# Two layers of a graph network on one core: g and y in one room, 64 bytes apart, and the start addresses of y and W modulo 512 bytes

## The chip, the cores and the metric

The kernel runs on one core of one Trainium2 chip. The time is the device time of one execution in microseconds; a kernel's figure is the median of several executions. Beside it there is one profiled execution, whose span runs from the first to the last instruction of the program. TensorE is called PE, VectorE DVE, ScalarE ACT, GpSimd POOL and SyncE SP, as in the profile.

## The reference

The input x has 64 batches of 256 rows and 512 features; adj is one 256 x 256 matrix of zeros and ones for all batches. There are two layers, each with a layer norm, a ReLU and a residual:

```
h   = relu(layernorm(x))
q, k, v = h @ Wq.T, h @ Wk.T, h @ Wv.T
rel = adj.T * (q @ k.T)                  # 256 x 256 for each batch
rel = rel / norm(rel, axis=2)            # each row by its length
x   = x + rel @ v

h   = relu(layernorm(x))
x   = x + (adj @ h) @ weight + bias
```

All of it is float32.

## The kernel before

**Arithmetic.** Every product of float32 operands is made of three passes: an operand is split into an upper part u, a lower part l and a third s, and a product is u by u, plus l by l, plus s by s, with a scaling of the bank by ScalarE (line 354, or 670 for the first pair) between the second pass and the third. A room of parts is therefore three tiles, such as `w_u`, `w_l`, `w_s`. The transform q times k is folded: m is the product of Wq and Wk, made once, and g = m times h, so that the scores are g times h.

**Stages.** Two batches (512 rows) make one pair, and there are 32 pairs; all loops are unrolled in Python. For one pair, in the kernel's own names:

- G (`g_stage`): g from m and h, 48 matmuls of 512 columns. The result is split into the parts of `gy`.
- V (`v_stage`): v from h and wv, 48 matmuls of 512 columns. The result goes into the rooms `v_low` and `late`.
- scores: g and h, 48 matmuls of 256 columns. VectorE multiplies the bank with the turned adj (line 433), and ScalarE takes the sums of squares (line 438).
- attend: the turned scores (`rel`) and the parts of v, 24 matmuls of 512 columns.
- gather: y = adj times the second layer's h, 32 matmuls of 256 columns. The result is split (lines 267 to 270) into the parts of `gy`, where g was.
- mix: y and W, 48 matmuls of 512 columns, onto a bank that ScalarE has filled with the bias (line 347).

Gather and mix belong to the pair before: in step i the order on PE is G(i), V(i), scores(i), gather(i-1), the rest of V(i), mix(i-1), attend(i). The last step has mix(i-1) behind attend(i), and then gather(i) and mix(i).

**Order.** `unit` puts two passes of a product on PE and hands the third to the next unit, so that the third pass stands behind the first two of the product that follows. A stage's first matmuls therefore alternate with the last ones of the stage ahead. Each piece of work goes to a `Plan` with its engine, a cost, and keys that it reads and writes; `Plan.order` works out due times back from PE's sequence and sorts every engine's work by a list schedule. The order is then fixed, and the framework sets the semaphores from the regions of the tiles that each instruction reads or writes.

**Operands.** Each matmul has a left operand, which is loaded into the array by an instruction of its own (a row PEld in the profile), and a right operand, which streams through it. `mm(out, left, right, first)` on line 248 issues both. In G the left operand is m and the right one h, in V h and wv, in scores g and h, in attend rel and v, in gather the second layer's h and adj, in mix y and W.

**Places.** The rooms are laid one behind the other in each partition, each size rounded up to 32 bytes. Most rooms are whole multiples of 512 bytes. In this text the place of an operand is its start modulo 512 bytes, counted from the start of `m`, `wv`, `h`, `v_low`, `late` and `rel`, which all have place 0. The small rooms (`ones`, `low_max`, `low_any`, the statistics and `norms`) take 928 bytes, and a filler makes this 1088, so that the rooms laid behind it stand at place 64; a second filler brings later rooms back to place 0:

```
    room("behind", 40)
    w_p = parts_room("w", DC, D)
    wq_sb, wk_sb = room("wq_sb", DC, D, tag="gy_u"), room("wk_sb", DC, D, tag="gy_l")
    gy_s = room("gy_s", DC, T, dtype=F32R)
    room("level", 112)
```

So before the change W, g and y all have place 64, the turned adj has place 448 (line 698 starts it 64 bytes ahead of a multiple), and every other operand has place 0. Within each of the kernel's tiles one 128-column block is 512 bytes, so an operand's place does not change with the block that is read.

Of the kernel before, what the change touches and what calls it, by code (L numbers as in the profile page):

```python
# [10 lines left out]
F32R = mybir.dt.float32r  # L11
I32 = mybir.dt.int32
# [101 lines left out]
def kernel(  # L114
# [12 lines left out]
    P = 128  # L127
    B, N, D = x.shape
    DC = D // P
    NC = N // P  # L130
    NB = 2
    TC = NB * NC
    T = NB * N
# [6 lines left out]
    pool = ctx.enter_context(tc.tile_pool(name="pool", bufs=1))  # L140
    ps_m = ctx.enter_context(tc.tile_pool(name="ps_m", bufs=1, space=bass.MemoryType.PSUM))

    def room(name, *shape, dtype=F32, tag=None):
        return pool.tile([P, *shape], dtype, name=name, tag=tag or name)

    def parts_room(name, *shape, tag=None):
        return [room(f"{name}_{k}", *shape, dtype=F32R, tag=f"{tag or name}_{k}") for k in "uls"]
# [8 lines left out]
    def hp(k, d):  # L156
        return h[k][:, d] if k < 2 else h_s[d // 2][:, d % 2]
    adj_low = room("adj_low", 2, D, tag="rel_u")
    v_low = room("v_low", 4, D, dtype=F32R)
    blocks = room("blocks", TC, DC, P)  # L160
    h_rel = room("h_rel", TC, D)
    bias_bc = room("bias_bc", D)
    wv_sb, w_sb = blocks.rearrange("p c d n -> p c (d n)"), ring[1]
    ident = room("ident", P)
    ones = room("ones", 1)
    wq_last, wk_last = room("wq_last", D), room("wk_last", D)
    low_max, low_any = room("low_max", 1), pool.tile([1, 1], I32, name="low_any")

    rooms = {}

# [32 lines left out]
    def place(plan, src, dst, keys_in, name, lands, early=0.0):  # L203
        width = src.shape[1] // J
        for j in range(J):
            for k in range(J):
                plan.add("SP", 0.65, lambda j=j, k=k: SP.dma_start(
                    out=dst[ts(j, S), ts(k, width)], in_=src[ts(k, S), ts(j, width)]),
                    keys_in, [(name, j, k)], lands=lands, early=early)

    stats = [
        [
            (room(f"st{j}{n}", TC, 6), room(f"mv{j}{n}", TC, 2), room(f"rs{j}{n}", TC), room(f"nb{j}{n}", TC))
            for n in range(2)
        ]
        for j in range(2)
    ]
    norms = [room(f"rn{n}", NB, NC) for n in range(2)]

    room("behind", 40)
    w_p = parts_room("w", DC, D)
    wq_sb, wk_sb = room("wq_sb", DC, D, tag="gy_u"), room("wk_sb", DC, D, tag="gy_l")
    gy_s = room("gy_s", DC, T, dtype=F32R)
    room("level", 112)

    V, A, G, SP = nc.vector, nc.scalar, nc.gpsimd, nc.sync
    count = {"bank": 0}
# [20 lines left out]
    MM, HALF = 0.231, 0.1185  # L250
# [3 lines left out]
    def split_right_ps(plan, ps, key, parts, names, at, cost=0.49):  # L254
        key = key if isinstance(key, list) else [key]
        u, l, s = ((lambda p=p: p(at)) for p in parts)
        ku, kl, ks = names
        plan.add("ACT", cost, lambda: A.activation(u(), ps, AF.Copy, scale=NEAR), key, ku)  # L258
        plan.add("DVE", 0.63, lambda: V.scalar_tensor_tensor(  # L259
            s(), f(u()), ONE, ps, op0=ALU.mult, op1=ALU.subtract), [*key, *ku], ks)  # L260
        plan.add("DVE", 0.6, lambda: V.scalar_tensor_tensor(  # L261
            l(), f(s()), -CROSS, f(u()), op0=ALU.mult, op1=ALU.add), [*ku, *ks], kl)
# [123 lines left out]
    def gy_half(b):  # L386
        return lambda k, d: [("gy_" + "uls"[k], d, b)]

    def gy_both(d):
        return [[("gy_" + k, d, b) for b in range(NB)] for k in "uls"]  # L390

# [2 lines left out]
    def g_stage(plan, i):  # L394
        for e in range(DC):
            first, second = three(
                lambda k, d, e=e: m_p[k][:, d, ts(e, P)], hp,
                named("m_u", "m_l", "m_s"), h_named, MM)
            unit(plan, first, second, lambda ps, key, e=e: split_right_ps(
                plan, ps, key, [lambda at, q=q: q[:, at, :] for q in gy],  # L400
                gy_both(e), e))

    held = []
# [14 lines left out]
    def scores(plan, i):  # L418
        rn = norms[i % 2]
        for b in range(NB):  # L420
            def outs_of(ps, k, d, b=b):
                return [
                    (ps[:, ts(n, N)], gy[k][:, d, ts(b * NC + n, P)], hp(k, d)[:, ts(b, N)])
                    for n in range(NC)
                ]
            first, second = three(None, None, gy_half(b), h_named, 2 * HALF, outs_of)

            def drain(ps, key, b=b):
                dst = plain[:, b].rearrange("p k (t j s) -> p k t j s", t=NC, j=J) if by_pe(i) else rel[:, b]

                def columns(part):
                    return part.rearrange("p (k t j s) -> p k t j s", k=NC, t=NC, j=J)
                plan.add("DVE", 0.6, lambda: V.tensor_mul(
                    *(part.rearrange("p k t j s -> p (k t) j s") for part in (
                        dst, columns(ps), columns(f(adjt[0]).rearrange("p k m -> p (k m)")))),),
                    [key, "adjt"], [("h_rel", b)])
                for k in range(NC):
                    plan.add("ACT", 0.53, lambda k=k: A.activation(
                        columns(ps)[:, k], dst[:, k], AF.Square, accum_out=rn[:, b, k : k + 1]),
                        [("h_rel", b)], [key, (f"rn{i % 2}", b, k)])  # L440
            unit(plan, first, second, drain)
# [91 lines left out]
    def gather(plan, i, exact):  # L533
        right = adjt[0]
        for b in range(NB):
            for d0 in range(0, DC, 2):
                def first(ps, b=b, d0=d0):
                    def go():
                        for m in range(NC):
                            c = b * NC + m  # L540
                            lefts = [late(3 + 2 * c + k) for k in range(2)] if exact else [
                                changing("late", "h2", 8, D)[:, c]]
                            for n, left in enumerate(lefts):
                                for d in range(2):
                                    mm(ps[:, ts(d, N)], left[:, ts(d0 + d, P)], right[:, m, :],
                                       d == 0 and m == 0 and n == 0)
                    needs = ["adjt", *(
                        ("late", r) for m in range(NC) for c in [b * NC + m]
                        for r in ((3 + 2 * c, 4 + 2 * c) if exact else (4 + c,)))]
                    yield 8 * HALF if exact else 8 * 0.216, go, needs  # L550

                def drain(ps, key, b=b, d0=d0):
                    split_left_ps(
                        plan, ps.rearrange("p (d n) -> p d n", d=2), key,
                        [lambda at, q=q: q[:, d0 : d0 + 2, ts(b, N)] for q in gy],
                        [[(f"gy_{k}", d0, b), (f"gy_{k}", d0 + 1, b)] for k in "uls"], None)
                unit(plan, first, None, drain)

    def mix(plan, i, blocks_of=range(4)):
        slot = i % 2  # L560
        for c in blocks_of:
            b = c // NC
            first, second = three(
                lambda k, d, c=c: gy[k][:, d, ts(c, P)], lambda k, d: w_p[k][:, d, :],
                gy_half(b), named("w_u", "w_l", "w_s"), MM, fresh_bank=False)

            def drain(ps, key, c=c):
                plan.add("DVE", 0.6, lambda: V.tensor_add(
                    ring[slot][:, c, :], ps, ring[slot][:, c, :]), [key], [(f"x{slot}", c)])
                if i + 1 == NP:  # L570
                    plan.add("SP", 0.65, lambda: SP.dma_start(
                        out=outs[i][:, c, :], in_=ring[slot][:, c, :]), [(f"x{slot}", c)], [], lands=3.0)
            unit(plan, first, second, drain, on=bias_bc)
# [53 lines left out]

    with tc.manual_schedule(engines=in_order):
        before_pairs()
    gy = [*(room(f"gy_{k}", DC, T, dtype=F32R) for k in "ul"), gy_s]  # L630
    rel_p = [room(f"rel_{k}", NB, NC, NC, P, dtype=F32R) for k in "ul"]
    adjt = []
    inexact = nc.values_load(low_any[0:1, 0:1], min_val=0, max_val=P * 0xFFF)
# [27 lines left out]
    def first_g(plan):  # L661

        banks = [next_bank() for _ in range(DC)]
        for k in range(3):
            for e, (ps, key) in enumerate(banks):
                def go(e=e, k=k, ps=ps):
                    for d in range(DC):
                        mm(ps, m_p[k][:, d, ts(e, P)], hp(k, d), k == 0 and d == 0)
                if k == 2:
                    plan.add("ACT", 0.49, lambda ps=ps: A.activation(ps, ps, AF.Copy, scale=ONE), [], [key])  # L670
                plan.add("PE", 4 * MM, go, [
                    *((("m_u", "m_l", "m_s")[k], d) for d in range(DC)), *((("h_u", "h_l", "h_s")[k], d) for d in range(DC))], [key])
        for e, (ps, key) in enumerate(banks):
            split_right_ps(plan, ps, key, [lambda at, q=q: q[:, at, :] for q in gy], gy_both(e), e)

    def turn_wv(plan):
        for d in range(DC):
# [105 lines left out]
```

## Time and profile before

| | |
|---|---|
| median of 3 runs | 1564.24 us (1563.73 to 1565.1) |
| the profiled execution | 1564.82 us, span 1563.0 us |
| PE busy | 1550.2 us, 99% of the span, 8046 matmuls |
| DVE busy | 1355.9 us, 87% |
| ACT busy | 1022.5 us, 65% |
| POOL busy | 24.4 us, 2% |
| DMA engines | 98 GB/s on average |
| granted PE clock | 1.0 |

A line of the timeline has the start in us from the span's start, the duration in us, the engine, the line of the kernel, the operation, and its tiles as output<-operands, with "xN" where N neighbours are merged into one line. In the names of this profile the right operand stands first: `bank<-w_u,gy_u` is a matmul of mix, with y as its left operand. All matmuls but the few transposes stand on line 248, the helper `mm`, so a stage is known by its tiles: `m_` with `h_` or `hs` is G, `wv_` is V, `gy_` with `h_` is scores, `rel_` is attend, `adjt` is gather and `w_` with `gy_` is mix. The duration of a merged line is not a sum that can be added to the next start, because matmuls overlap in the record; the difference of two starts is used instead.

### The profile page before, as it was taken

To read this page: it belongs to the slowest core of one execution; us is meant where nothing else is said; L and a number is where in the kernel's file an instruction comes from. 1 tells how busy PE (TensorE), PEld (TensorE's weight loads), DVE (VectorE), ACT (ScalarE), POOL (GpSimd) and SP (SyncE) were. 2 spreads that over 40 slices of the span, in tenths; PEclk is the share of its full clock that TensorE was granted. 3 is DMA by queue.
4 is the path that set the end of the run, shared out by engine and by line. 5 is a ranking of instruction groups with operands and counts; after the bars stand their busy time and mean duration, and the time that the engine had idled before them with its cause. 6 is when DMAs were issued, how large, how long until landed. Compare 5 with 4: busy or idle time off the path is not lost.

```text
span 1563.0 us, 22543 instructions
## 1 busy us (share of the span) xinstructions
PE 1550.2 (99%) x8046; PEld 1322.6 (85%) x8046; DVE 1355.9 (87%) x2419; ACT 1022.5 (65%) x1941; POOL 24.4 (2%) x39
## 2 busy tenths in 40 slices
PE   8999999999999999999999999999999999999998
PEld 5788888888888888888888888888888888888886
DVE  6997889898889988898988899888989888988776
ACT  5567666676667676666676676766666766666654
POOL 0000000000000000000000000000000000000000
PEclk9999999999999999999999999999999999999999
DMA  5321333223333223333223332233332233322211
GB/s 197 113 82 42 121 111 120 71 75 112 117 114 119 64 77 119 113 117 87 73 98 118 111 122 68 77 114 114 115 108 70 80 122 111 119 69 77 86 55 56
DMA packets 91112, 153.63 MB, mean 98 GB/s; under 512 B 17136, under 2 KB 32240, under 8 KB 90992
## 3 DMA queue, kind: packets, MB, share of 16 engines
q1 hardware_dynamic: 80768, 116.46, 24.7%
q0 software_dynamic: 8432, 32.51, 5.8%
q10 hardware_dynamic: 1792, 3.15, 0.6%
q8 instruction: 65, 1.06, 0.3%
q14 instruction: 55, 0.45, 0.1%
HBM read 70.78 MB, written 33.55 MB: 67 GB/s over the span
## 4 chain that ended last, share of the span: by engine, by line
PE 95%; DVE 3%; DMA 0%; ACT 0%; issue 0%; DVEq 0%
PE bank L248 95%; DMA fresh<-in_x_dram 0%; DVE late_parts L259 0%; DVE late_parts L261 0%; DVE rel_s_parts L459 0%; DVE st L285 0%; DVE gy_l L268 0%; DVE rel_l L464 0%; DVE wv_l L261 0%; DVE m_l L261 0%; DVE ht L315 0%; DVE wv_s L259 0%; DVE m_s L259 0%; DVE w_l L261 0%; DVE h_l L332 0%
## 5 line engine op out<-in xcount | busy, mean ns | idle before, releaser
L354 ACT ACTIVATE bank<-bank 128x512 f32<-128x512 f32 x572 | 333.1, 582 | 312.2 <-PE bank L248 307.7
L248 PE MATMUL bank<-wv_s,hs 128*128 128x512 f32 x512 | 138.6, 392 | 0.0
L248 PE MATMUL bank<-w_u,gy_u 128*128 128x512 f32 x512 | 138.0, 391 | 0.0
L248 PE MATMUL bank<-wv_u,h_u 128*128 128x512 f32 x512 | 137.6, 390 | 0.0
L248 PE MATMUL bank<-w_l,gy_l 128*128 128x512 f32 x512 | 137.4, 390 | 0.0
L248 PE MATMUL bank<-w_s,gy_s 128*128 128x512 f32 x512 | 137.2, 390 | 0.0
L248 PE MATMUL bank<-wv_l,h_l 128*128 128x512 f32 x512 | 136.9, 389 | 0.0
L248 PE MATMUL bank<-h_l,m_l 128*128 128x512 f32 x512 | 136.6, 389 | 0.1
L248 PE MATMUL bank<-h_u,m_u 128*128 128x512 f32 x512 | 136.5, 389 | 0.0
L248 PE MATMUL bank<-hs,m_s 128*128 128x512 f32 x512 | 136.3, 389 | 0.0
L259 DVE SCALAR_TENSOR_TENSOR gy_s<-gy_u,bank 128x512 fp32r<-128x512 f32 x128 | 86.3, 676 | 43.0 <-ACT gy_u L258 43.0
L248 PEld LDWEIGHTS bank<-w_u,gy_u 128*128 128x128 f32 x512 | 96.0, 188 | 20.8
L248 PEld LDWEIGHTS bank<-w_l,gy_l 128*128 128x128 f32 x512 | 96.1, 188 | 20.7
L248 PEld LDWEIGHTS bank<-h_l,m_l 128*128 128x128 f32 x512 | 96.0, 188 | 20.4 <-DVE h_l L332 0.5
L248 PEld LDWEIGHTS bank<-wv_l,h_l 128*128 128x128 f32 x512 | 96.1, 188 | 20.2
L248 PEld LDWEIGHTS bank<-h_u,m_u 128*128 128x128 f32 x512 | 96.0, 188 | 20.2 <-ACT m_u L258 0.2
L248 PEld LDWEIGHTS bank<-w_s,gy_s 128*128 128x128 f32 x512 | 96.0, 188 | 20.3 <-ACT bank L354 0.2
L248 PEld LDWEIGHTS bank<-hs,m_s 128*128 128x128 f32 x512 | 96.1, 188 | 19.9
L248 PE MATMUL bank<-adjt_r,late_parts 128*128 128x256 f32 x896 | 112.6, 277 | 0.0
L248 PEld LDWEIGHTS bank<-wv_s,hs 128*128 128x128 f32 x512 | 93.8, 188 | 19.3 <-ACT bank L354 0.9
L248 PEld LDWEIGHTS bank<-wv_u,h_u 128*128 128x128 f32 x512 | 93.7, 188 | 17.8
L248 PEld LDWEIGHTS bank<-adjt_r,late_parts 128*128 128x128 f32 x896 | 107.3, 188 | 0.0
(110 smaller groups left out, 3071.7 us busy)
## 6 DMA issues: line engine op xcount, KB each, us to landing
fresh<-in_x_dram SPq DMA_DIRECT2D x31, 1024.0 KB, 5.7
blocks<-h_rel SPq DMA_DIRECT2D x496, 64.0 KB, 2.0
x_ring<-in_x_dram SPq DMA_DIRECT2D x31, 1024.0 KB, 7.8
out_dram<-x_ring POOLq DMA_DIRECT2D x31, 1024.0 KB, 5.4
h_rel<-h_rel SPq DMA_DIRECT2D x464, 32.0 KB, 1.8
x_ring<-in_L_gnn_weight_dram SPq DMA_DIRECT2D x1, 1024.0 KB, 12.8
blocks<-in_L_gnn_Wv_dram ACTq DMA_DIRECT2D x1, 1024.0 KB, 10.8
out_dram<-x_ring SPq DMA_DIRECT2D x4, 256.0 KB, 2.3
```

What stands on the lines that cost most here:

```text
L248: nc.tensor.matmul(out, left, right, start=first, stop=True, skip_group_check=True)
L259: plan.add("DVE", 0.63, lambda: V.scalar_tensor_tensor(s(), f(u()), ONE, ps, op0=ALU.mult, op1=ALU.subtract), [*key, *ku], ks)
L354: plan.add("ACT", 0.49, lambda: A.activation(ps, ps, AF.Copy, scale=ONE), [], [key])
```

## The change

- The parts of W are laid directly behind `h_rel`, at place 0.
- Each of the three `gy` rooms gets 16 more elements (64 bytes). y is the view from the room's start, at place 0; g is the view from element 16 on, at place 64. `as_y` and `as_g` make these views of a flat tile, and `gy` is no longer used as an operand by name, but as `y_p` and `g_p`.
- The statistics, `norms`, `ones` and `low_max` are laid between the `gy` rooms, so that each `gy` room starts at place 0 again; `bias_bc`, `ident` and the last rows of Wq and Wk follow `gy_s` and move by 96 bytes in place. The filler `behind` is gone and `level` is smaller; the rooms laid behind it keep their addresses.
- Because g and y now overlap with a shift, a block of y covers a part of two blocks of g. Gather's split gets extra keys `g_u`, `g_l` and `g_s`, and scores reads them beside `gy_`, so that the plan knows that a block of y waits for both halves of g that it covers.

No instruction is added or removed, and no shape changes.

```diff
+    wv_sb, w_sb = blocks.rearrange("p c d n -> p c (d n)"), ring[1]
+    BEHIND = 16
+    w_p = parts_room("w", DC, D)
+
+    def as_y(tile):
+        return tile[:, : DC * T].rearrange("p (d t) -> p d t", d=DC)
+
+    def as_g(tile):
+        return tile[:, BEHIND : BEHIND + DC * T].rearrange("p (d t) -> p d t", d=DC)
...
+    wq_room = room("wq_sb", DC * T + BEHIND, tag="gy_u")
+    stats = [norm_rooms(0)]
+    norms = [room(f"rn{n}", NB, NC) for n in range(2)]
+    wk_room = room("wk_sb", DC * T + BEHIND, tag="gy_l")
+    stats.append(norm_rooms(1))
+    ones, low_max = room("ones", 1), room("low_max", 1)
+    gy_s = room("gy_s", DC * T + BEHIND, dtype=F32R)
+    wq_sb, wk_sb = as_y(wq_room), as_y(wk_room)
...
+    room("level", 104)
...
-    room("behind", 40)
-    w_p = parts_room("w", DC, D)
-    wq_sb, wk_sb = room("wq_sb", DC, D, tag="gy_u"), room("wk_sb", DC, D, tag="gy_l")
-    gy_s = room("gy_s", DC, T, dtype=F32R)
-    room("level", 112)
...
+    def g_half(b):
+
+        return lambda k, d: [(name + "uls"[k], d, b) for name in ("gy_", "g_")]
...
-                plan, ps, key, [lambda at, q=q: q[:, at, :] for q in gy],
+                plan, ps, key, [lambda at, q=q: q[:, at, :] for q in g_p],
...
-                    (ps[:, ts(n, N)], gy[k][:, d, ts(b * NC + n, P)], hp(k, d)[:, ts(b, N)])
+                    (ps[:, ts(n, N)], g_p[k][:, d, ts(b * NC + n, P)], hp(k, d)[:, ts(b, N)])
...
-            first, second = three(None, None, gy_half(b), h_named, 2 * HALF, outs_of)
+            first, second = three(None, None, g_half(b), h_named, 2 * HALF, outs_of)
...
-                        [lambda at, q=q: q[:, d0 : d0 + 2, ts(b, N)] for q in gy],
-                        [[(f"gy_{k}", d0, b), (f"gy_{k}", d0 + 1, b)] for k in "uls"], None)
+                        [lambda at, q=q: q[:, d0 : d0 + 2, ts(b, N)] for q in y_p],
+                        [[(f"gy_{k}", d, b) for d in (d0, d0 + 1)] + [
+                            (f"g_{k}", *((d, 0) if b else (d - 1, 1))) for d in (d0, d0 + 1)] for k in "uls"], None)
...
-                lambda k, d, c=c: gy[k][:, d, ts(c, P)], lambda k, d: w_p[k][:, d, :],
+                lambda k, d, c=c: y_p[k][:, d, ts(c, P)], lambda k, d: w_p[k][:, d, :],
...
-    gy = [*(room(f"gy_{k}", DC, T, dtype=F32R) for k in "ul"), gy_s]
+    gy = [*(room(f"gy_{k}", DC * T + BEHIND, dtype=F32R) for k in "ul"), gy_s]
+    g_p, y_p = [as_g(part) for part in gy], [as_y(part) for part in gy]
```

More of the change, by code (lines that the diff above doesn't have):

```diff
@@ L161, with norm_rooms @@
     h_rel = room("h_rel", TC, D)
+    wv_sb, w_sb = blocks.rearrange("p c d n -> p c (d n)"), ring[1]
[5 more added lines that the diff above has]
+        return tile[:, BEHIND : BEHIND + DC * T].rearrange("p (d t) -> p d t", d=DC)
+    def norm_rooms(j):
+        return [(room(f"st{j}{n}", TC, 6), room(f"mv{j}{n}", TC, 2), room(f"rs{j}{n}", TC), room(f"nb{j}{n}", TC))
+                for n in range(2)]
+    wq_room = room("wq_sb", DC * T + BEHIND, tag="gy_u")
[6 more added lines that the diff above has]
+    wq_sb, wk_sb = as_y(wq_room), as_y(wk_room)
+    low_any = pool.tile([1, 1], I32, name="low_any")
     bias_bc = room("bias_bc", D)
-    wv_sb, w_sb = blocks.rearrange("p c d n -> p c (d n)"), ring[1]
     ident = room("ident", P)
-    ones = room("ones", 1)
     wq_last, wk_last = room("wq_last", D), room("wk_last", D)
-    low_max, low_any = room("low_max", 1), pool.tile([1, 1], I32, name="low_any")
+    room("level", 104)
     rooms = {}
@@ L209, in place @@
                     keys_in, [(name, j, k)], lands=lands, early=early)
[L211 to L218, printed above, removed]
-    room("behind", 40)
-    w_p = parts_room("w", DC, D)
-    wq_sb, wk_sb = room("wq_sb", DC, D, tag="gy_u"), room("wk_sb", DC, D, tag="gy_l")
-    gy_s = room("gy_s", DC, T, dtype=F32R)
-    room("level", 112)
     V, A, G, SP = nc.vector, nc.scalar, nc.gpsimd, nc.sync
@@ L673, in first_g @@
         for e, (ps, key) in enumerate(banks):
-            split_right_ps(plan, ps, key, [lambda at, q=q: q[:, at, :] for q in gy], gy_both(e), e)
+            split_right_ps(plan, ps, key, [lambda at, q=q: q[:, at, :] for q in g_p], gy_both(e), e)
     def turn_wv(plan):
```

## The prediction

> **What bounds the kernel now.** I read the page first: the busy shares, the granted clock and the chain that ended last.
>
> ```profile
> PE 1550.2 (99%) x8046; PEld 1322.6 (85%) x8046; DVE 1355.9 (87%) x2419; ACT 1022.5 (65%) x1941; POOL 24.4 (2%) x39
> ...
> PEclk9999999999999999999999999999999999999999
> ...
> PE 95%; DVE 3%; DMA 0%; ACT 0%; issue 0%; DVEq 0%
> ```
>
> PE is busy 99% of the span at full clock and makes 95% of the chain. VectorE is next, at 87%, with idle time in every step. So the time is the sum of the distances between the starts of successive matmuls, and the question is whether the change alters any of those distances. Next I read the timeline of PE over one whole step, of 47.5 us.
>
> ```profile
> 782.62 1.07 PE L248 MATMUL bank<-hs,m_s 128*128 128x512 f32 x4
> ...
> 793.50 1.07 PE L248 MATMUL bank<-wv_s,hs 128*128 128x512 f32 x4
> ...
> 808.30 1.07 PE L248 MATMUL bank<-wv_s,hs 128*128 128x512 f32 x4
> 809.20 1.09 PE L248 MATMUL bank<-w_u,gy_u 128*128 128x512 f32 x4
> 810.13 1.09 PE L248 MATMUL bank<-w_l,gy_l 128*128 128x512 f32 x4
> 811.05 1.10 PE L248 MATMUL bank<-wv_s,hs 128*128 128x512 f32 x4
> 811.98 1.09 PE L248 MATMUL bank<-w_u,gy_u 128*128 128x512 f32 x4
> 812.91 1.07 PE L248 MATMUL bank<-w_l,gy_l 128*128 128x512 f32 x4
> ...
> 819.26 1.07 PE L248 MATMUL bank<-w_s,gy_s 128*128 128x512 f32 x4
> 820.16 0.62 PE L248 MATMUL bank<-v_low,rel_u 128*128 128x512 f32 x2
> ...
> 821.08 1.08 PE L248 MATMUL bank<-w_s,gy_s 128*128 128x512 f32 x4
> 822.00 0.61 PE L248 MATMUL bank<-v_low,rel_u 128*128 128x512 f32 x2
> ...
> 826.08 1.07 PE L248 MATMUL bank<-h_u,m_u 128*128 128x512 f32 x4
> ```
>
> The reader is to take differences of starts. From 782.62 to 793.50 there are 12 groups of four, or 48 matmuls in 10.88 us: 226.7 ns each. G passes into V in this stretch, so both operands change rooms, and no distance grows. All of these operands have place 0. From 812.91 to 819.26, inside mix, 7 groups of four take 6.35 us: again 226.8 ns each. There both operands have place 64. What costs more is the passage between the two places. V's third pass at 808.30 still takes 0.90 us, the first two groups of mix 0.93 and 0.92, the late V group among them 0.93, and the group after that again 0.93, against 0.907 for four at 226.7 ns. Where mix meets attend, 821.08 to 822.00 takes 0.92. From attend to the next G, which share place 0, nothing is added.
>
> **What the Trainium skill says.** Perfetto Trace Analysis, section Tensor Engine Instruction (MATMUL, LD_WEIGHTS), says that a matmul's end in the profile is estimated. The 1.07 us of a group beside a distance of 0.907 agrees, so I use starts alone. TensorE: Matmul & The Clock Gate, in Wait — 56ns, not 53.3ns?, gives 215.7 ns from start to start for 512 columns at full clock. The trace has 226.7, which decides. The same page, under Step-by-step: what each phase is for, says that loading the next weights takes no read bandwidth from the running matmul, through a second port. The trace does not fit this fully: the distance depends on where the operands stand. No page that I found states a rule on places modulo 512 bytes, so the cost comes from the trace alone.
>
> **The change part by part.**
>
> *Mix at place 0.* The step from 809.20 to 826.08 holds 12 groups of four from mix, one of V and 22 matmuls of attend, 74 in all. At 226.7 ns they would take 16.77 us; they take 16.88. The excess is 0.107 us, from the unrounded starts. About 0.08 of it lies in the passage from V, and about 0.025 in the passage to attend. I took the same sum for every step: 30 steps have mix between V and attend. 27 of them give 0.107 to 0.108 us, and three give less, 0.101, 0.093 and 0.083: in these PE was held shortly before mix. Together they come to 3.2 us. With y and W at place 0, these passages become of the kind that G to V is, at no excess. All of this is on PE, on the path. **Minus 3.2 us.**
>
> *The last step* has mix behind attend. Its entry into mix at 1530.95 and the attend group within cost 0.05 us over 226.7 ns each. Then gather and mix alternate; over their own undisturbed distances (113.3 and 226.7 ns) these cost 0.2 us, and a passage from place 0 to gather at 448 and back remains (from gather to V it costs 0.015 us). I take half: 0.1, with 0 and 0.2 as ends. **Minus 0.15 us in all.**
>
> *What stays.* In scores g at 64 meets h at 0, as before, at 117.6 ns for 256 columns; gather's operands keep 0 and 448. The passages from V to scores, and from gather to V, are untouched. No more is to be had there: zero.
>
> *The parts of the small rooms.* `ident`, `bias_bc` and the last rows of Wq and Wk move by 96 bytes in place. `ident` streams through PE 60 times in the whole kernel (groups of 16, 24, 16 and 4). If each cost what the dearest passage matmul does, 240 against 226.7 ns, that is 13 ns by 60, or 0.8 us; at the beginning PE waits for others, and such a loss lies partly beside those waits. The lower end is a gain of about as little. I take zero, with plus 0.8 and minus 0.2 as ends. ScalarE's reads of `bias_bc`, and the splits' writes, take 588 and 590 ns now at places 0 and 64, so no cost of a place shows there: zero.
>
> *The waits from the overlap.* y of rows b and block d covers g of the other half too. So the split of gather's first unit must now wait until scores of b=1 has read its g. The first two passes of it stand before gather on PE, so u and l wait for nothing new. The third pass stands from 800.98 to 801.92, and the writer that needs it is the third part, L269.
>
> ```profile
> 802.19 0.69 DVE L433 TENSOR_TENSOR h_rel<-bank,adjt_r 128x512 f32<-128x512 f32 x1 [1.10 <-PE bank L248]
> 803.41 0.69 DVE L268 TENSOR_TENSOR gy_l<-bank,gy_u 128x512 fp32r<-128x512 f32 x1 [0.53 <-ACT gy_u L267]
> ...
> 805.22 1.27 DVE L269 SCALAR_TENSOR_TENSOR gy_s<-gy_l,bank 128x512 fp32r<-128x512 f32 x2
> ...
> 807.01 1.29 DVE L268 TENSOR_TENSOR gy_l<-bank,gy_u 128x512 fp32r<-128x512 f32 x2
> ```
>
> VectorE's row 433 has waited for that same pass and stands 3 us ahead of 805.22 on the same engine, so the new wait is met before it is reached: zero. In the plan the third part could start two operations (0.49 and 0.6 us) behind gather's end, and the third pass of scores costs 0.95 us there, so no order should move. G's split over the y of the pair before is likewise behind PE work that its own bank already waits for. If the cover were gone, what is queued behind is the splits of v and then mix's first groups at 809.20.
>
> **The sum.** Minus 3.2, minus 0.15, plus 0, is minus 3.3 us. The profiled execution would go from 1564.82 to 1561.5. It stands 0.6 above the median of the runs, 1564.24, and all terms are differences on PE, so I take them from the median: **1560.9 us**. For this kernel 0.2%, which is 3.1 us, is about what a measurement can tell from no change; the forecast lies just beyond that.
>
> **The rivals.** *The passage stays in part or whole.* The excess may belong to the change of rooms or to a third pass that alternates with another product, not to the place. For it: each excess sits at such a seam. Against it: G's seams with V and with attend have the same alternation, change the same number of rooms and cost 0 to 1 ns in all. If only the entry from V goes, the gain is 30 by 0.08, 2.4 us: 1561.8. If only the seam with attend goes, it is 30 by 0.025: 1563.5. If nothing goes, because the rooms don't come to lie where the text says, 1564.2. The rooms' sizes, rounded up to 32 bytes, come out even at W and each gy room, so I hold that unlikely.
>
> *Slower: the flat room is tracked as one piece.* If a write of one block of y waited for a read of another block of the same part, ScalarE's fourth split (L267) would wait for VectorE's third L268. It starts ahead of it now:
>
> ```profile
> 806.86 0.60 ACT L267 ACTIVATE gy_u<-bank 128x512 fp32r<-128x512 f32 x1
> 807.34 0.60 ACT L354 ACTIVATE bank<-bank 128x512 f32<-128x512 f32 x1
> ```
>
> The third L268 begins at 807.01 and runs 0.65 to 0.69, so the split would begin at about 807.7, 0.8 us late, and the scaling behind it (L354) would end at 808.8, where V's third pass on PE wants it at 808.30. PE would lose 0.5 us in each of 30 steps: plus 15, less 3.3, gives 1576. It decides from a delay of about 0.35 us on, the time between the scaling's end at 807.94 and 808.30. Against it: each block is a region of its own, and even if a strided block counted from its first to its last byte, the fourth split's stretch would not touch the third's, as they cover different blocks d.
>
> **How the numbers follow.** That the passages go whole: 0.80; the gain is then 3.1 to 3.6 us, and two thirds of it, with the runs' own spread of 1.4 us, lies beyond 3.1. In part: 0.08. Not at all: 0.05. Slower: 0.07. So faster by over 0.2%: 0.8 by 0.67 and a little, 0.55; within 0.2%: 0.27 from the main case and 0.11 from the two rivals with the smaller gain, 0.38; slower 0.07. The range goes from 1559.8 (3.6 and the runs' spread) to 1562.6, which takes in the partial case and the bound on `ident`; about 0.17 is left out.
>
> **What would show it.** In the timeline of PE the distance from the first group of mix to the G after it should be 16.77 instead of 16.88 us, all groups of four at 0.906 or 0.907, and V to mix as even as G to V. Scores should stay at 117.6 ns. The counts of instructions should be the same, and the order on ACT and DVE as well. If L269 or L267 of gather start later and L354 before V's third pass ends after PE wants it, the slower rival is right. If mix's first groups keep 0.93, the place is not the cause.

## The result and the profile after

The changed kernel takes 1562.11 us, median of 18 runs (1560.41 to 1562.96), against 1564.22 for the kernel before (18 runs, 1563.51 to 1565.48). The ratio is 0.9982, with a 95% interval of 0.9976 to 0.9989. The whole interval lies below 1, so the changed kernel is faster, by 1.7 to 3.8 us; the ratio itself stays within 0.2%, which this text called the bound of a measurement. The means differ by 2.7 us. In a second comparison (e9 below) the ratio is 0.9981 (0.9973 to 0.9989) and the medians are 1561.35 and 1564.70.

First the page of the profile after: the busy shares and the chain that ended last. Line 255 is the helper `mm`, formerly 248.

```profile
PE 1548.2 (99%) x8046; PEld 1323.5 (85%) x8046; DVE 1355.3 (87%) x2419; ACT 1022.7 (66%) x1941; POOL 24.3 (2%) x39
...
PE 95%; DVE 3%; DMA 1%; ACT 0%; issue 0%; ACTq 0%; DVEq 0%
```

Little on this page tells the kernels apart: the busy time of PE is 2.0 us smaller, and the counts are the same. Then the timeline of PE in the changed kernel, over the same kind of stretch as before. Starts are to be subtracted.

```profile
853.71 1.07 PE L255 MATMUL bank<-wv_s,hs 128*128 128x512 f32 x4
854.62 1.07 PE L255 MATMUL bank<-w_u,gy_u 128*128 128x512 f32 x4
855.52 1.07 PE L255 MATMUL bank<-w_l,gy_l 128*128 128x512 f32 x4
856.43 1.07 PE L255 MATMUL bank<-wv_s,hs 128*128 128x512 f32 x4
857.34 1.07 PE L255 MATMUL bank<-w_u,gy_u 128*128 128x512 f32 x4
858.24 1.07 PE L255 MATMUL bank<-w_l,gy_l 128*128 128x512 f32 x4
...
866.40 1.07 PE L255 MATMUL bank<-w_s,gy_s 128*128 128x512 f32 x4
867.31 0.61 PE L255 MATMUL bank<-v_low,rel_u 128*128 128x512 f32 x2
...
871.39 1.07 PE L255 MATMUL bank<-h_u,m_u 128*128 128x512 f32 x4
```

Every group of four is now 0.90 or 0.91 us from the next, at the entry into mix, where V's late third pass stands among mix's first groups, and where mix meets attend. From 854.62 to 871.39 the 74 matmuls of mix and attend take 16.77 us, or 226.6 ns each; before they took 16.88.

To weigh this over the whole run I use one number for each trace: **the step**, from the first matmul of one mix to the first of the next, as the median over 29 steps. It leaves out the start, the last step and the few steps in which PE is held up by something else. Before it is 47.540 us, after 47.433: 0.107 us less.

The two profiled executions differ by more, 1564.82 to 1560.76; the second of these is the fourth fastest of its 18 runs. From the traces, the difference comes from three stretches. The first mix begins at 96.08 us before and at 95.06 after, which is 1.02 earlier. No passage of mix lies in that stretch, and it varies from run to run: the first G starts between 26.1 and 27.1 us in the 14 traces of this text, and e1 below, which has the small rooms at the places they had before, has its first mix at 94.82. From the first mix to the thirtieth it is 1379.21 and 1376.27, which is 2.94 less in 29 steps. From there to the last matmul it is 0.11 less. So about 3.1 us are the change, and about 1 us of that pair is most likely chance.

### The profile page after: what moved, and what is told of

It is laid out like the page before. It is cut to its first block, busy times and chain, and to the rows that moved or that the text cites. A ratio compares the mean times of both kernels' runs of the same rounds, so it can differ in the third digit from the quotient of the medians.

```text
span 1559.0 us, 22543 instructions
## 1 busy us (share of the span) xinstructions
PE 1548.2 (99%) x8046; PEld 1323.5 (85%) x8046; DVE 1355.3 (87%) x2419; ACT 1022.7 (66%) x1941; POOL 24.3 (2%) x39
## 4 chain that ended last, share of the span: by engine, by line
PE 95%; DVE 3%; DMA 1%; ACT 0%; issue 0%; ACTq 0%; DVEq 0%
PE bank L255 95%; DMA bias_bc<-in_L_gnn_bias_dram 1%; DMA x_ring<-in_x_dram 1%; DVE late_parts L266 0%; DVE late_parts L268 0%; DVE rel_s_parts L470 0%; DVE st L292 0%; DVE rel_l L475 0%; DVE gy_l L275 0%; DVE m_l L268 0%; DVE gy_l L268 0%; DVE wv_l L268 0%; DVE ht L322 0%; DVE wv_s L266 0%; DVE m_s L266 0%
```

## The experiments

All of them keep the work of the kernel and change where rooms lie. In all 14 traces the sequence of operations and tiles is the same on PE, DVE, ACT and POOL, so the plan's order has not moved anywhere, and on every engine the traces before and after hold the same number of waits for each semaphore. The table gives the step, and how far three stretches of it exceed even distances (226.67 ns for 512 columns, 113.33 for 256), as medians in ns: mix with attend, the stretch from the first scores to the last gather, and the rest of V. What is left of the step, from G to the first scores, changes by at most 9 ns. The time is that of one run, for the kernel before and after that of the profiled one; as comparisons of the kernels these single times are worth less than the step.

| kernel | places: y, W, g, adj | step us | mix, attend | scores to gather | rest of V | time us |
|---|---|---|---|---|---|---|
| before | 64, 64, 64, 448 | 47.540 | 108 | 273 | 15 | 1564.82 |
| after | 0, 0, 64, 448 | 47.433 | 0 | 273 | 15 | 1560.76 |
| e1 | 64, 0, 64, 448 | 47.807 | 374 | 273 | 15 | 1571.98 |
| e2 | 0, 64, 64, 448 | 47.640 | 207 | 273 | 15 | 1567.62 |
| e3 | 64, 64, 128, 448 | 47.633 | 108 | 359 | 15 | 1567.28 |
| e4 | 0, 0, 0, 448 | 47.500 | 0 | 339 | 15 | 1564.08 |
| e5 | 0, 0, 448, 448 | 47.461 | 0 | 299 | 16 | 1562.89 |
| e6 | 0, 0, 32, 448 | 47.460 | 0 | 290 | 16 | 1561.49 |
| e7 | 32, 32, 96, 448 | 47.607 | 125 | 310 | 24 | 1565.56 |
| e8 | 256, 256, 320, 448 | 47.434 | 0 | 273 | 15 | 1560.76 |
| e10 | 0, 0, 64, 0 | 47.620 | 0 | 447 | 28 | 1566.70 |
| e11 | 128, 128, 192, 448 | 47.520 | 55 | 299 | 21 | 1564.69 |
| e12 | 0, 0, 48, 448 | 47.547 | 0 | 372 | 23 | 1564.32 |

**e1: W alone at 0.** In the kernel before, `w_p` is laid ahead of the small rooms.

```diff
+    w_p = parts_room("w", DC, D)
     bias_bc = room("bias_bc", D)
...
-    w_p = parts_room("w", DC, D)
```

> The kernel before with the parts of W alone laid at place 0; y and g stay at 64. Theory A (an operand pair at two places costs on every matmul, and passages cost on top): mix now pairs y at 64 with W at 0, as scores pairs g at 64 with h at 0. From scores (117.6 against 113.3 ns per load) mix gains 3 to 5 ns per matmul, 230 to 232 ns inside it, 4.5 to 7 us over 1536 matmuls, less the passages' 3.2: 1565 to 1569. Rival B (the gain of the change came from somewhere else than the places of the two operands together, such as W's move alone): mix stays at 226.7 ns and the time is 1561 to 1562.

The timeline of PE inside mix:

```profile
814.83 1.09 PE L248 MATMUL bank<-w_u,gy_u 128*128 128x512 f32 x4
815.76 1.10 PE L248 MATMUL bank<-w_l,gy_l 128*128 128x512 f32 x4
816.69 1.09 PE L248 MATMUL bank<-w_s,gy_s 128*128 128x512 f32 x4
817.62 1.10 PE L248 MATMUL bank<-w_u,gy_u 128*128 128x512 f32 x4
```

Three groups take 2.79 us: 232.5 ns per matmul here, and 233.3 on average inside mix. Mix pays inside its own groups too, not only at the seams. The step is 0.267 us longer than before, and one run took 1571.98. W's move alone loses; the size, 6.6 ns per matmul, is above the 3 to 5 expected, and so is the time.

**e2: y alone at 0.** In the changed kernel W is pushed on by 64 bytes.

```diff
+    room("push", 16)
     w_p = parts_room("w", DC, D)
+    room("pull", 112)
```

> The changed kernel with the parts of W at place 64; y stays at 0, g at 64. Theory A: a pair at two places, W 64 bytes behind y; 3 to 5 ns per matmul inside mix if it costs as scores do, 0 to 1 ns if it costs as gather does; passages to V and attend come back in part. 1562 to 1569. Rival B (y's move alone was enough): mix at 226.7 ns with even passages, 1561 to 1562.

The timeline of PE inside mix:

```profile
816.03 1.08 PE L257 MATMUL bank<-w_u,gy_u 128*128 128x512 f32 x4
...
818.77 1.08 PE L257 MATMUL bank<-w_u,gy_u 128*128 128x512 f32 x4
```

Three groups take 2.74 us, 228.3 ns per matmul. This too is slower than before, by 0.1 us a step. So neither half of the change brings anything; y and W have to go together. In mix the sign of the distance matters: over even distances, the loaded operand at the higher place (e1) costs 6.6 ns per matmul of mix on average, the streamed one at the higher place (e2) 2.9.

**e3: the whole change, moved on by 64 bytes.** The shared rooms, views, keys and the order of the small rooms stay; y and W stand together at 64 again.

```diff
+    room("push", 16)
     w_p = parts_room("w", DC, D)
...
-    room("level", 104)
+    room("level", 88)
```

> The changed kernel with W, y and g all moved on by 64 bytes: y and W at 64 together, g at 128; the shared rooms, their views and all waits as in the changed kernel. Theory A: the passages between V, mix and attend cost 0.10 to 0.11 us per step again, 3.2 us in all, inside mix 226.7 ns. Scores with g at 128 is unknown: between 113.3 and 122 ns for each of 1536, minus 6.7 to plus 6.7 us. Rival B (sharing the room, or the moved small rooms, made the gain): passages stay even.

The timeline of PE at V's passage into mix:

```profile
809.42 1.07 PE L256 MATMUL bank<-wv_s,hs 128*128 128x512 f32 x4
810.32 1.09 PE L256 MATMUL bank<-w_u,gy_u 128*128 128x512 f32 x4
811.25 1.09 PE L256 MATMUL bank<-w_l,gy_l 128*128 128x512 f32 x4
812.17 1.10 PE L256 MATMUL bank<-wv_s,hs 128*128 128x512 f32 x4
813.11 1.09 PE L256 MATMUL bank<-w_u,gy_u 128*128 128x512 f32 x4
814.03 1.07 PE L256 MATMUL bank<-w_l,gy_l 128*128 128x512 f32 x4
```

V's group at 809.42 takes 0.90 us, the next four take 0.93, 0.92, 0.94 and 0.92: the picture of the kernel before. Mix and attend exceed even distances by 108 ns, exactly as before. This shows that the gain comes from the place of y and W, and not from the shared room, its waits or the new order of the small rooms. Scores lose as well with g at 128 (119.9 ns on average).

**e4: g at 0 too.** Fillers keep every other room at its place.

```diff
-    BEHIND = 16
+    BEHIND = 0
...
+    room("fill0", 16)
     wk_room = room("wk_sb", DC * T + BEHIND, tag="gy_l")
...
+    room("fill1", 16)
     gy_s = room("gy_s", DC * T + BEHIND, dtype=F32R)
...
-    room("level", 104)
+    room("level", 120)
```

> The changed kernel with g at place 0 as well (BEHIND = 0), so that only the turned adj stands elsewhere (448). Theory A1 (only unequal places cost): scores go from 117.6 to 113.3 ns per matmul and the passages V to scores and back become even, minus 6 to 7 us: 1555. Theory A2 (matmuls of 256 columns need their two streams apart, since a load is 188 ns long and longer than one of them streams): scores rise above 117.6, to 120 to 130 ns, plus 4 to 19 us: 1565 to 1580.

The timeline of PE at the first scores:

```profile
793.97 1.12 PE L257 MATMUL bank<-h_u,gy_u 128*128 128x256 f32 x8
794.92 1.12 PE L257 MATMUL bank<-h_l,gy_l 128*128 128x256 f32 x8
795.88 1.09 PE L257 MATMUL bank<-wv_s,hs 128*128 128x512 f32 x4
```

Eight matmuls take 0.95 and 0.96 us, 119 to 120 ns each, against 117.6 with g at 64; most distances in scores are 120 ns, and the mean is 119.1. So what suits 512 columns does not suit 256: A1 is wrong. A2 has the direction right, but the loss is smaller than its range: the step is 0.067 us longer than the changed kernel's, and the run took 1564.08 instead of 1565 or more. The reason that A2 gave, the length of a load, is not shown by this.

**e10: the turned adj at 0 too.** The same question for gather.

```diff
-        adjt[:] = [turned_adj[:, P - 16 : P - 16 + NC * N].rearrange("p (c n) -> p c n", c=NC)]
+        adjt[:] = [turned_adj[:, : NC * N].rearrange("p (c n) -> p c n", c=NC)]
```

> The changed kernel with the turned adj at place 0 as well, so that gather's two operands share a place. Scores took 120 ns per matmul of 256 columns with both operands at 0, 117.6 with them 64 apart. If 256 columns want the two apart in general, gather goes from 113.3 to about 120 ns, plus 6 to 7 us less some of the passages into V: 1566 to 1568. If gather is even at one place, as the matmuls of 512 columns are, its passages vanish: minus 0.5 to 1 us, 1560 to 1561.

The timeline of PE in gather:

```profile
802.86 2.80 PE L255 MATMUL bank<-adjt_r,late_parts 128*128 128x256 f32 x22
805.50 0.86 PE L255 MATMUL bank<-wv_u,h_u 128*128 128x512 f32 x3
```

22 matmuls take 2.64 us: 120 ns each, as most of the distances in scores with both operands at 0, where the changed kernel's gather takes 113.3. The step is 0.187 us longer, and 1566.70 lies in the range of the first of the two expectations.

**e5, e6, e12: other places for g.** e5 swaps the two views, so that g is 64 ahead of y, and lays each room at 448; e6 is e4 with 8 elements; e12 starts g 12 elements on.

```diff
e5
+    room("ahead", 112)
     def as_y(tile):
-        return tile[:, : DC * T].rearrange("p (d t) -> p d t", d=DC)
+        return tile[:, BEHIND : BEHIND + DC * T].rearrange("p (d t) -> p d t", d=DC)
     def as_g(tile):
-        return tile[:, BEHIND : BEHIND + DC * T].rearrange("p (d t) -> p d t", d=DC)
+        return tile[:, : DC * T].rearrange("p (d t) -> p d t", d=DC)
...
-                            (f"g_{k}", *((d, 0) if b else (d - 1, 1))) for d in (d0, d0 + 1)] for k in "uls"], None)
+                            (f"g_{k}", *((d + 1, 0) if b else (d, 1))) for d in (d0, d0 + 1)] for k in "uls"], None)
e6
-    BEHIND = 16
+    BEHIND = 8
e12
     def as_g(tile):
-        return tile[:, BEHIND : BEHIND + DC * T].rearrange("p (d t) -> p d t", d=DC)
+        return tile[:, 12 : 12 + DC * T].rearrange("p (d t) -> p d t", d=DC)
```

> The changed kernel with g 64 bytes ahead of y (g at 448, y and W at 0): views swapped, each room starting at 448. Mix and its passages as in the changed kernel: 226.7 ns. Theory C (what counts is how far the loaded operand lies from the streamed one, with its sign): in mix W 64 ahead of y cost 2.1 ns per matmul where y 64 ahead of W cost 6.4, so scores with g 64 behind h should cost about 2 ns over 113.3, some 115 instead of 117.6, minus 4 us: 1558 on the profiled run. Theory D (any unequal place costs scores the same): 117.6 ns, 1561 to 1562.

> The changed kernel with g at 32 instead of 64; y and W at 0. Scores took 120 ns per matmul with g at 0, 117.6 at 64 and 120.4 at 128. If the cost goes smoothly with the distance, 118 to 119 ns here, plus 1 to 2 us over the changed kernel; if only whole steps of 64 bytes count, 120 ns as at 0, plus 2.5 us (or 117.6, as at 64). Mix and its passages at 226.7 ns in each case.

> The changed kernel with g 48 bytes behind y instead of 64 (y and W at 0). Scores with their passages and gather's cost 0.339 us per step over even distances with g at 0, 0.290 at 32, 0.273 at 64 and 0.31 at 96 (with y at 32). If there is a better place between 32 and 64, it is here: 0.25 to 0.27, a step of 47.41 to 47.43 us and at most 0.7 us in all; if 64 is the best of its neighbourhood, 0.273 to 0.29 and a step of 47.43 to 47.45.

Mix stays even in all three. e5: scores take 118.0 ns, not 115, so theory C, carried over from mix, is wrong. e6: 118.3 ns on average, with single distances between 115 and 123; the step is 0.027 us longer, a little less than the smooth theory had it. e12 does not fit a smooth cost: with g at 48 scores keep their pace to within 0.5 ns, but gather, whose operands have not moved, goes from 113.3 to 117.8 ns. The first two lines are of the changed kernel, the other two of e12:

```profile
847.57 2.66 PE L255 MATMUL bank<-adjt_r,late_parts 128*128 128x256 f32 x22
850.07 1.08 PE L255 MATMUL bank<-wv_u,h_u 128*128 128x512 f32 x4
...
849.64 2.75 PE L255 MATMUL bank<-adjt_r,late_parts 128*128 128x256 f32 x22
852.23 1.09 PE L255 MATMUL bank<-wv_u,h_u 128*128 128x512 f32 x4
```

The 22 matmuls take 2.50 us in the first and 2.59 in the second. In e12 every gather settles at 117.8 ns. The same slower pace stands in the traces of the kernels before and after, where no place differs between the steps: of the first 31 gathers, 29 settle at 113.3 ns and two at 117.8, and the 32nd, which stands behind mix instead of scores, takes 117.8 as well. So gather has two paces at the same addresses, and a stage's pace does not depend on its own places alone. In e7 and e11, where y and W stand at 32 and 128, the 32nd gather takes 113.3 ns, with its own places unchanged, so what stands ahead of gather has a part in it; the traces do not show how. None of these places beats g at 64.

**e7, e11, e8: the change moved on by 32, 128 and 256 bytes.** As e3, with 8, 32 and 64 elements; e8 is shown.

```diff
+    room("push", 64)
     w_p = parts_room("w", DC, D)
...
-    room("level", 104)
+    room("level", 40)
```

> The changed kernel with W, y and g moved on by 32 bytes: y and W at 32 together, g at 96. Inside mix 226.7 ns. Theory A with a cost by distance: the passages V to mix and mix to attend cost about half of their 0.107 us per step, 0.05, 1.5 us in all. Theory A with a cost by steps of 64 bytes: either none of it (0) or all of it (3.2 us). Scores with g at 96: 118 to 120 ns, plus 0 to 4 us.

> The changed kernel with W, y and g moved on by 128 bytes: y and W at 128, g at 192. Moved on by 256 bytes the kernel kept its step of 47.43 us. If the place counts modulo 128, the step is 47.43 us again and the passages have no excess; if modulo 256, the passages cost 0.10 to 0.13 us per step as with 32 and 64 bytes, and scores with g at 192 (the same distance from 256 as 64 ahead) take about the 118 ns of g at 448: a step of 47.55 to 47.62 us.

> The changed kernel with W, y and g moved on by 256 bytes: y and W at 256, g at 320. Whether the place counts modulo 512 or modulo a part of it. If modulo 256 or less: the step stays at the changed kernel's 47.43 us, mix to attend without excess and scores at 117.6 ns. If modulo 512 or more: the passages come back, at 0.10 to 0.13 us per step as with 32 and 64 bytes, 3 to 4 us in all, and scores with g at 320 take something else than 117.6 ns.

The timeline of PE in e8, at V's passage into mix and at the seam with attend:

```profile
900.95 1.07 PE L256 MATMUL bank<-wv_s,hs 128*128 128x512 f32 x4
901.85 1.07 PE L256 MATMUL bank<-w_u,gy_u 128*128 128x512 f32 x4
902.76 1.07 PE L256 MATMUL bank<-w_l,gy_l 128*128 128x512 f32 x4
...
913.64 1.07 PE L256 MATMUL bank<-w_s,gy_s 128*128 128x512 f32 x4
914.55 0.62 PE L256 MATMUL bank<-v_low,rel_u 128*128 128x512 f32 x2
```

With 256 bytes between them and the rest, y and W pass as evenly as at 0, and the step is 47.434 us. With 32 it costs 125 ns, with 64 108, with 128 55. So at the places tried the cost repeats after 256 bytes and not only after 512, and it is not in proportion to the distance. Neither e7's 125 ns nor e11's 55 was expected: the theories had none, half or all of 107 for e7, and 100 to 130 for e11. In all of these runs V, attend and G stay at 0, so whether it is the place itself that costs, or only the difference from the neighbours, has not been separated.

**e9: the changed kernel once more,** with 15 runs beside 19 of the kernel before.

> The changed kernel unchanged, for a second profile and for rounds beside the kernel before on one chip. If the places are all that differs, the steps without a stall again take 47.43 us against 47.54, 3.2 us over 30 steps, and the ratio lies at 0.998. The first profile had stalls of PE in V's third pass (waiting for ScalarE's scaling) of 0.7 us in all, against 0.55 before; if these come at random they are between 0.1 and 2 us again; if the shorter step makes them, they are above 0.7.

The step is 47.434 us again, the ratio 0.9981 (0.9973 to 0.9989). Some steps are longer than the median, by stalls in V's third pass or in the scores, and now and then by a gather at the slower pace. Summed over the 29 steps this is 1.2 us in this trace, 0.7 in the first of the same kernel and 0.6 before. Over all traces these steps are few, and the sum is between 0.1 us (e1) and 2.1 us (e11). They are real time, and they make a single run's comparison uncertain by more than 1 us. Some of them recur: the 15th step is 0.44 and 0.42 us longer than the median in the two traces of the changed kernel and 0.02 to 0.54 longer in eight others, but not in the traces of the kernel before, e1, e2 and e3; the kernel before has a like one, 0.41, in its 28th step. That the shorter step makes them more frequent is neither shown nor excluded: the smallest sum goes with the longest step, but the two profiles of the same kernel already differ by 0.5.

No version beats the changed kernel; e8 equals it.

## Why the prediction was right, point by point

**What bounds it, and mix at place 0.** Right, and to the nanosecond: 0.107 us per step was predicted from the seams of the trace before, and the step fell by 0.107. Both parts of the seam went, from V and to attend. e3 brings exactly these 108 ns back.

**The last step.** This term was mis-sized: 0.15 us were expected and nothing came. The entry into mix there did become even (from 49 ns of excess to none), as the prediction had it. But the other 0.1 us rested on the wrong pace for gather. The prediction took 113.3 ns as gather's undisturbed distance there and put the rest down to passages. The last gather takes 117.8 ns throughout, first before and then after the change:

```profile
1543.52 2.76 PE L248 MATMUL bank<-adjt_r,late_parts 128*128 128x256 f32 x22
1546.12 1.07 PE L248 MATMUL bank<-w_u,gy_u 128*128 128x512 f32 x4
...
1539.40 2.75 PE L255 MATMUL bank<-adjt_r,late_parts 128*128 128x256 f32 x22
1542.00 1.09 PE L255 MATMUL bank<-w_u,gy_u 128*128 128x512 f32 x4
```

Both stretches take 2.60 us. Over its 32 matmuls gather exceeds 113.3 ns by 142 ns in both kernels, so about two thirds of the 0.2 us that the prediction counted was gather's own slower pace and no passage. And the last 47 matmuls of mix now exceed even distances by 92 ns instead of 47, which takes back what the entry brings. The half that I took for the removable part was a guess, and it was wrong; why the last mix got slower has not been found.

**`ident` and the small rooms.** Zero was right: the transposes stand 109 ns apart (median) before and after.

**The waits from the overlap, and the slower rival.** Zero was right. Counted from the first group of mix, gather's fourth split by ScalarE (L267, L274 after the change) starts 2.49 us ahead before and 2.50 after (medians), and VectorE's third L268 (now L275) 2.33 and 2.34 ahead. The split is not held until that L268 has ended, so the rival that the flat room is tracked as one piece is excluded.

**The rival that the passage stays.** Excluded by the even groups in the timeline after, and by e3. The time alone could not have done it: 1562.11 is nearer to 1561.8, the forecast for the case in which only the entry from V goes, than to 1560.9.

**The sum.** 3.3 us were forecast, 3.1 to 3.2 are there on PE (29 steps and the last), and the medians show 2.1 in one comparison and 3.35 in the other, the means 2.7 and 3.0. The first median, 1562.11, is 1.2 above the forecast of 1560.9, and it lies in the part of the range that had been left for the partial case; that the number agrees to this extent is in part luck, while the mechanism is shown by the step. The cause of the difference between 2.1 and 3.35 has not been settled; the beginning, which varies by 1 us, and the stalls are large enough for it.

**The bound.** The better chance went to a gain beyond 0.2%; both comparisons lie just within it. With an effect at the bound itself that was a coin's toss.

## What to carry to other kernels

When PE is the bound and hardly waits, look at the distances between the starts of its matmuls. Here two passages between products that are even in themselves cost 0.1 us a step, and moving the start addresses of one product's two operands took that away. Move an operand pair as a whole and check both widths: here 512 columns did best with all operands at one place, while for 256 columns 64 bytes between the two was the best of the places tried in scores, and both 0 and 128 were worse; in mix, moving one operand of the pair alone lost 0.27 or 0.10 us a step, where moving both gained 0.11. For an effect of 0.1 us in a step of 47, the step's median in one trace gives the size that 18 runs leave open between 1.7 and 3.8 us.

## What was not expected of the hardware

- The pace of matmuls depends on the start addresses, and y and W at 256 equal those at 0 (a step of 47.434 and 47.433 us); at 128 they cost half as much as at 64 (55 and 108 ns a step), and at 32 more (125). The reason inside the chip is open.
- A pair at two places cost by sign in mix: 233.3 ns per matmul of 512 columns with the loaded operand's place 64 bytes higher, 229.6 with the streamed one's, as means over mix, and 226.7 with both at 0.
- 256 columns with both operands at 0 take 120 ns in gather and in most distances of scores (119.1 on average there). Scores take 117.6 with g at 64 and 119.9 with g at 128; gather takes 113.3 in most steps with adj at 448. Why gather gets to 113.3 and scores do not is open.
- The same gather, at the same places, runs at 113.3 or 117.8 ns: at 117.8 in every step of e12, and in two gathers and the last one of the kernels before and after.
